# A graph-attention and GraphSAGE kernel: who divides by the softmax sum, when the list decoder's right sides are made, and which queue stores the last row

## The chip, the cores and the metric

The kernel runs on one core of a Trainium2 chip, as one launch. The metric is the device time in microseconds (us) of that launch. Each core has a matrix engine (TensorE, in the profile PE), a vector engine (VectorE, DVE), an activation engine (ScalarE, ACT), GpSimd (POOL) and SyncE (SP). Each has its own queue of instructions, which it works through in order. DMA transfers are issued from the queues of SP, ACT and POOL.

## The reference

The input is a table `x` of 4096 nodes by 512 features and a matrix `adj` of 4096 by 4096 int32, in which about one entry in a thousand is 1. Two layers follow each other, each with a residual sum and a layer norm.

```python
# layer 0: graph attention, 8 heads of 64
Wh = jnp.einsum('nf,hfo->hno', x, W)
f1 = jnp.einsum('hno,ho->hn', Wh, a[:, :F_OUT]);  f2 = ... a[:, F_OUT:]
e = jax.nn.leaky_relu(f1[:, :, None] + f2[:, None, :], ALPHA)
e = jnp.where(adj[None, :, :] > 0, e, NEG_INF)
out = jnp.einsum('hnm,hmo->hno', jax.nn.softmax(e, axis=-1), Wh)
x = _layernorm(x + out)
# layer 1: mean over the neighbours, then three linear maps
agg = (adj > 0) @ x / jnp.maximum(deg, 1.0)
y = concatenate([x @ W_self + b_self, agg @ W_nb + b_nb]) @ W_comb + b_comb
x = _layernorm(x + relu(y))
```

## The kernel before, in words

The 4096 nodes are cut into 32 blocks of 128. Because `adj` is almost empty, the kernel does not multiply by it: it turns each row of `adj` into a short list of neighbour numbers and gathers the neighbours' rows from a table in device memory. (A dense version stands behind a flag and is not entered on this input.)

**Stage 1** (the loop at line 951, counter `b`, and what follows to line 1027). For each block TensorE transposes `x` (`transposed`, line 354) and multiplies it with the weights in two halves (`node_half`, line 375); VectorE copies each half from PSUM into a tile `row` (line 379), and `store` (line 947) writes the row of `Wh`, with its attention terms, to the table `t0`. Rows 0 to 30 are stored from POOL's queue. The last, row 31, is stored at line 980 from ACT's queue, where it stands behind the masks of the last `adj` block (`mask_adj`, line 428). SP's queue carries the loads of `adj` (1 MB each, tile `at`). Behind its last one stands `load_late` (line 928), a load of 1 MB into the tile `m1` for one of the three `adj` blocks that are handled later.

Lists are decoded for four blocks at a time by the generator `decode` (line 464). It yields between pieces, and `some(lists)` runs one piece: four pieces for each `b` in stage 1. Its sixteen pieces are, in order: three of bit work, four of maxima, the count of neighbours (which makes `nx`, line 504), two empty ones, piece 11 with a small product on TensorE (line 511) and the first of four selection matrices (lines 520 and 521), three more of these, piece 15 with the right side `lq` (line 525), the products of the four selections with it (line 531) and all that reads them (lines 535 to 548), and piece 16 with the owner table (line 550).

**Stage 2**, layer 0 (the loop at line 1035, counter `i` from -3 to 33; here "pass i"). It is a pipeline over blocks, written out by hand. Every engine's order is the order of these calls:

- TensorE: `a_shared(i+1)` (line 694, the weighted sums of the gathered rows of block i+1), then a decoder product if a piece has one, `a_z(i-1)` (line 739, block i-1 times a folded weight), `transposed(i)` (line 354), and on some even passes the fold of a late `adj` block (line 447).
- POOL: five row gathers for block i+6 (line 621). There are five gather buffers, so they wait for `a_shared(i+1)`.
- VectorE: `a_weights(i+3)` (lines 652, 653), `a_weigh(i+2)` (line 669, the long one), `a_recip(i+1)` (line 702), `a_first(i+2)` (line 677), `a_own_sum(i+2)` (line 687), the second half of `a_scale(i+1)` (line 710), a piece of the decoder on passes -2 to 4 and from 9 on, `a_moments(i+1)` (line 717, the sum with x).
- ScalarE: `root(i)` and `norm(i)` (lines 725 to 734), the first half of `a_scale(i+1)` (line 708, four operations of 64 columns), `a_exp(i+3)` (lines 659, 660), a cast of owners (line 648), copies of the product of `a_z` (line 743) and of the transposed block (line 360), and on even passes up to 8 the mask of a late half block (line 943), after which SP issues the next load into the single tile `m1`.

Two PSUM facts matter in this stage. The exponentials `ew` have one buffer, so `a_exp(i+3)` waits until `a_own_sum(i+2)` has read the last ones. Decoder products and transposed blocks share one buffer, `tp`.

**Stage 3**, layer 1 (line 1156), gathers rows of a second table `t1`, which `a_z` has filled, and multiplies on TensorE (lines 765 and 772).

Of the kernel before, what the change touches and what calls it, by code (L numbers as in the profile page):

```python
# [36 lines left out]
OP = mybir.AluOpType  # L37
# [3 lines left out]
P = 128  # L41
# [72 lines left out]
def listed_layers(  # L114
# [15 lines left out]
    nc = tc.nc  # L130
    N, FIN = x.shape
    H, _, D = w0.shape
    NB = N // P
    FB = FIN // P
    HD = H * D
    HH = HD // 2
# [327 lines left out]
    def decode(b0, dp, place):  # L464
# [40 lines left out]
        dg = dp.tile([P, G], F32, name="dg", bufs=1)  # L505
        nc.vector.tensor_scalar(dg, deg[:, bs], 1.0, None, OP.max)
        nc.vector.reciprocal(L[:, :, KL + 1], dg)
        for k in range(3):
            yield
        po = ps.tile([P, G], F32, name="sm", bufs=2)  # L510
        nc.tensor.matmul(po, lhsT=triuq, rhs=nx, start=True, stop=True)
# [4 lines left out]
        for b in range(b0, b0 + G):  # L516
# [9 lines left out]
            lq, lst[:, bs, K0:].unsqueeze(2).to_broadcast([P, G, KH, EX + H]),  # L526
            part.unsqueeze(1).unsqueeze(3).to_broadcast([P, G, KH, EX + H]), OP.mult,
        )
        pe = ps.tile([P, G, KH, EX + H], F32, name="sm", bufs=2)
        for g in range(G):  # L530
            nc.tensor.matmul(
# [98 lines left out]
    def gather(table, b, g, at=None):  # L630
        for k in range(KS):
            rows_of(
                g[:, k, 0 : table.shape[1]], table, (idx if at is None else at)[:, b, k : k + 1]
            )
        return g

    def gather_early(b, pool):
        return gather(t1[0 : 2 + min(LE + b, LX) * P, :], b, pool, idxe)
# [5 lines left out]
    G0, OWN, E, RD, Y, NM, MV, RS = ({} for _ in range(8))  # L644

    def a_owners(b, wp):
        OWN[b] = wp.tile([P, KH, HP], F32, name="own", bufs=4)
        nc.scalar.copy(OWN[b], own[:, b])

    def a_weights(b, wp):  # L650
        e = E[b] = wp.tile([P, KS + 1, H], F32, name="e", bufs=3)[:, 0:KS]
        nc.vector.tensor_add(e, G0[b][:, :, 0:H], f1s[:, b])
        nc.vector.scalar_tensor_tensor(e, e, SLOPE, e, OP.mult, OP.max)
# [8 lines left out]
    def halves_of(t):  # L662
        return t[:, H : H + 2 * (2 * HH - H)].rearrange(
            "p (a c) -> p a c", a=2
        )[:, :, 0:HH]

    def a_weigh(b, sl):
        gv = G0[b][:, sl, H:TW].rearrange("p k (h d) -> p k h d", h=H)
        nc.vector.tensor_tensor(  # L669
            gv, gv, E[b][:, sl].unsqueeze(3).to_broadcast([P, sl.stop - sl.start, H, D]),  # L670
            OP.mult,
        )

    def a_first(b):

        NM[b] = ps.tile([P, 2 * HD], F32, name="num")
        nc.vector.tensor_tensor(
            halves_of(NM[b]).rearrange("p a (h d) -> p a h d", d=D),
            G0[b][:, 0, H:TW].rearrange("p (a h d) -> p a h d", a=2, d=D),
            E[b][:, 0].rearrange("p (a h) -> p a h", a=2).unsqueeze(3).to_broadcast(  # L680
                [P, 2, H // 2, D]
            ),
            OP.mult,
        )

    def a_own_sum(b):
        nc.vector.tensor_copy(NM[b][:, 0:H], E[b][:, 0])

    def a_shared(b):

        for a in range(2):
            r = slice(a * (H + HH), H + HH + a * HH)
            for k in range(KH):
                nc.tensor.matmul(  # L694
                    NM[b][ts(k, HP), a * HD : a * HD + r.stop - r.start],
                    lhsT=OWN[b][:, k, :], rhs=G0[b][:, K0 + k, r],
                    start=False, stop=True, tile_position=(0, k * HP), skip_group_check=True,
                )

    def a_recip(b, wp):  # L700
        RD[b] = wp.tile([P, H], F32, name="rd", bufs=2)
        nc.vector.reciprocal(RD[b], NM[b][:, 0:H])  # L702

    def a_scale(b):

        for h in range(H // 2):
            s = NM[b][:, H + h * D : H + (h + 1) * D]
            nc.scalar.mul(s, s, RD[b][:, h : h + 1])  # L708
        s = NM[b][:, HD : HD + HH].rearrange("p (h d) -> p h d", d=D)
        nc.vector.tensor_tensor(  # L710
            s, s, RD[b][:, H // 2 :].unsqueeze(2).to_broadcast([P, H // 2, D]), OP.mult
        )

    def a_moments(b, wp):
        Y[b] = wp.tile([P, HD], F32, name="y", bufs=2)
        mu = MV[b] = small.tile([P, 1], F32, name="ln_sum")
        nc.vector.scalar_tensor_tensor(
            Y[b].rearrange("p (a c) -> p a c", a=2), halves_of(NM[b]), 1.0,
            xs[:, b, :].rearrange("p (a c) -> p a c", a=2), OP.mult, OP.add, accum_out=mu,
        )  # L720

    def root(b, wide):

        rs = RS[b] = small.tile([P, 1], F32, name="ln_rs")
        nc.scalar.activation(  # L725
            wide, Y[b], AF.Square, bias=MV[b], scale=-float(HD), accum_out=rs
        )
        nc.scalar.activation(rs, rs, AF.Ln, bias=eps, scale=1.0 / HD**3)
        nc.scalar.activation(rs, rs, AF.Exp, scale=-0.5)
        nc.scalar.mul(MV[b], MV[b], -1.0 / HD)  # L730
        nc.scalar.mul(MV[b], MV[b], rs)

    def norm(b, to):
        nc.scalar.activation(to, Y[b], AF.Identity, bias=MV[b], scale=RS[b])  # L734
# [71 lines left out]
    def some(todo):  # L806
        for p in todo:
            next(p, None)
# [86 lines left out]
    def node_block(w, xT, between=None, keep=False):  # L895
        row = wp.tile([P, FW], F32, name="row", bufs=3)
        node_half(w, 0, xT, w_sb, row)
        if between is not None:
            fold_adj(between, dp)
            max_keys(between)  # L900
        node_half(w, 1, xT, w_sb, row)
        node_rest(w, row)
        if not keep:
            store(w, row, nc.gpsimd)
        return row
# [17 lines left out]
    def load_late():  # L923

        if late:
            b, h = late[0]
            r = b * P + h * (P // NH)
            nc.sync.dma_start(
                m1.bitcast(I32),
                adj[r : r + P // NH, :].rearrange("(j r) (s c) -> (r s) j c", r=RG, s=SEG),  # L930
            )
# [14 lines left out]
    def store(w, row, eng=nc.scalar):  # L946
        eng.dma_start(t0[2 + w * P : 2 + (w + 1) * P, :], row)

    w, lists = 0, []
    for b in range(LB):  # L950
# [11 lines left out]
        for k in range(1 + (b in AHEAD)):  # L962
# [7 lines left out]
            row = node_block(w, xT, None if k or nxt is None else b, keep=nxt is None)  # L970
            w, xT = w + 1, nxt
# [5 lines left out]
            next(pieces, None)  # L977
        if b % G == G - 1:
            lists = [decode(b + 1 - G, dp, on_own)]
    store(w - 1, row)  # L980
    load_late()
    xa_cm.__exit__(None, None, None)

# [33 lines left out]
    wq = ctx.enter_context(tc.tile_pool(name="work2", bufs=1))  # L1017
# [12 lines left out]
    def on(b):  # L1030
        return 0 <= b < NB
# [3 lines left out]
    for i in range(-3, NB + 2):  # L1035
        if on(i + 1):
            a_shared(i + 1)
        if on(i + 1 + GA):
            G0[i + 1 + GA] = gather(t0, i + 1 + GA, gps[(i + 1 + GA) % GA])
        elif on(i + GA - NB - 1) and i + GA - NB - 1 < GA:  # L1040
            b = i + GA - NB - 1
            G1[b] = gather_early(b, gps[(NB + b) % GA])
        if on(i + 3):
            a_weights(i + 3, wq)
        if on(i + 2):
            a_weigh(i + 2, slice(K0, KS))
        if on(i + 1):
            a_recip(i + 1, wq)
        if on(i + 2):
            a_first(i + 2)  # L1050
            a_own_sum(i + 2)
        if on(i):
            root(i, xs[:, i, :])
            norm(i, xs[:, i, :])
        if on(i + 1):
            a_scale(i + 1)
        if -3 < i <= 4 or i > TURN:
            some(lists)
            if i > TURN and i % 3 == 0:
                some(lists)  # L1060
        if i == 21:
            lists = [late_lists(dp, last)]
        if on(i + 1):
            a_moments(i + 1, wq)
        if on(i + 3):
            a_exp(i + 3)
        if i == -3:
            a_owners(0, wp)
        if on(i + 4):
            a_owners(i + 4, wp)  # L1070
        if i == -3:
            pieces(4, m2s)
        if i == -2:
            for _ in m2s:
                pass
        if on(i - 1):
            a_z(i - 1, XT.pop(i - 1), m2, wp)
        if on(i):
            XT[i] = transposed(i, wp)
            store_xT(i, XT[i])  # L1080
        if i > -3 and i % 2 == 0 and late:
            b, h = late[0]
            mask_late(lp)
            if h:
                key_bank(b)
                fold_adj(b, dp)
                max_keys(b)
        if i == TURN:
            lists = [chain(lists[0], decode(NB - G, dp, on_last))]
        if 2 <= i < 6:  # L1090
            next(biased)
        if i == TURN + 1:
            loaded = load_fold(0, w_self, m1, weight(fc, "wc"))
        if 16 <= i < 20:
            if i == 16:
                biased = fold_bias(loaded, bcol[:, 0:FB])
            next(biased)
        if i == 20:
            sum_bias()
# [479 lines left out]
```

## Time and profile before

| | |
|---|---|
| median of three runs | 668.76 us (667.65 to 668.82) |
| profiled execution | 669.31 us, of it 667.5 us span |
| TensorE busy | 564.3 us, 85% |
| ScalarE busy | 441.0 us, 66% |
| VectorE busy | 402.6 us, 60% |
| GpSimd busy | 353.4 us, 53% |
| mean granted TensorE clock | 0.951 |
| first gather of stage 2 | 214.07 us |
| first neighbour sum of stage 3 | 469.43 us |

The span runs from the first to the last instruction; the profiled execution's own time is 1.8 us longer. Busy shares are averages over three stages with different limits, so they say little alone: stage 1 runs to about 214 us, stage 2 to about 469 us, stage 3 to the end. A row of the list of waits has an engine and its line, what released it, the total in us, the number of times and the longest. A row of the timeline has start and duration in us, engine, line, operation, output and inputs, and in brackets the idle time of that engine before it.

### The profile page before, as it was taken

The page shows a single profiled execution, that of the slowest core. Times are in us where ns is not written, and L with a number is a line of the kernel's source. Part 1 is how long each engine was busy: PE and PEld are TensorE (multiplying, and loading weights), DVE is VectorE, ACT ScalarE, POOL GpSimd, SP SyncE. Part 2 cuts the span into 40 slices and gives each one's busy share as a digit, 9 for nine tenths or more (in the row PEclk, how much of TensorE's full clock was granted, in tenths as well). Part 3 has the DMA queues.
Part 4 walks back from the last instruction along what each step waited for, and adds up shares of the span by engine and source line. Part 5 has one row for each costly group of instructions (what it writes and reads, how often), then busy time and mean ns, then how long its engine had stood idle before and what let it go on. Part 6 is the DMA issues. An engine that isn't in the chain of part 4 may idle for free.

```text
span 667.5 us, 9452 instructions
## 1 busy us (share of the span) xinstructions
PE 564.3 (85%) x2562; PEld 282.4 (42%) x2562; DVE 402.6 (60%) x1214; ACT 441.0 (66%) x1152; POOL 353.4 (53%) x475
## 2 busy tenths in 40 slices
PE   4798889888897728686988679899899999999992
PEld 2466566656664303332433243444343333333320
DVE  7246858686786557676888968886014454454321
ACT  2687879788783247579788748697326566766443
POOL 5112121112113777567577757637776777777770
PEclk9989999999999957789899979999999999999996
DMA  8999999999997789889799979859978899989882
GB/s 250 406 408 408 410 407 408 409 408 400 390 360 282 211 278 322 301 279 345 253 388 316 302 212 301 279 196 299 316 232 279 301 323 315 336 309 327 296 248 101
DMA packets 92070, 210.45 MB, mean 315 GB/s; under 512 B 13726, under 2 KB 13734, under 8 KB 92010
## 3 DMA queue, kind: packets, MB, share of 16 engines
q1 hardware_dynamic: 63024, 114.05, 46.0%
q0 software_dynamic: 28656, 95.18, 44.2%
q10 hardware_dynamic: 330, 0.55, 0.2%
q8 instruction: 23, 0.38, 0.2%
q14 instruction: 37, 0.30, 0.1%
HBM read 175.91 MB, written 33.82 MB: 314 GB/s over the span
## 4 chain that ended last, share of the span: by engine, by line
PE 43%; DMA 23%; ACT 16%; DVE 9%; issue 4%; POOL 3%; SPq 1%; ACTq 0%; DVEq 0%; POOLq 0%
DMA at<-in_adj_dram 14%; PE pw L765 9%; PE nm L765 9%; PE pw L739 5%; PE pw L375 5%; DMA g<-t,idx 5%; PE pw L772 4%; ACT ab L428 4%; PE nm L772 3%; DMA m<-in_adj_dram 3%; ACT num L708 3%; POOL g L621 3%; PE tp L313 2%; DVE g L669 2%; ACT xs L734 2%
## 5 line engine op out<-in xcount | busy, mean ns | idle before, releaser
L621 POOL DMA_INDIRECT g<-t,idx x290 | 275.3, 949 | 115.2 <-issue 48.4
L375 PE MATMUL pw<-w_sb,xT 128*128 128x264 f32 x512 | 130.5, 401 | 6.6 <-issue 3.7
L428 ACT ACTIVATE ab<-at 128x2048 bf16<-128x2048 int32 x58 | 110.9, 1917 | 34.3 <-DMA at<-in_adj_dram 33.5
L739 PE MATMUL pw<-wr,xT 128*128 128x512 f32 x256 | 124.1, 629 | 7.2 <-ACT xT L360 7.1
L375 PEld LDWEIGHTS pw<-w_sb,xT 128*128 128x128 f32 x512 | 94.7, 194 | 33.6 <-issue 9.6
L382 POOL COPY lst<-row 128x8 f32<-128x8 f32 x32 | 8.6, 270 | 158.1 <-DVE row L379 136.6
L739 PEld LDWEIGHTS pw<-wr,xT 128*128 128x128 f32 x256 | 48.5, 200 | 70.1 <-issue 53.1
L669 DVE TENSOR_TENSOR g<-g,ew 128x2048 f32<-128x2048 f32 x32 | 72.9, 2279 | 0.0
L765 PE MATMUL nm<-m,xT 128*128 128x512 f32 x128 | 58.8, 602 | 0.0
L765 PE MATMUL pw<-m,xT 128*128 128x512 f32 x128 | 58.8, 602 | 0.0
L354 PE MATMUL tp<-ident,xs 128*128 128x128 f32 x256 | 40.6, 283 | 11.6 <-ACT xs L734 4.1
L708 ACT ACTIVATE num<-num,rd 128x64 f32<-128x64 f32 x128 | 36.7, 287 | 19.9 <-DVE rd L702 16.5
L379 DVE COPY row<-pw 128x264 f32<-128x264 f32 x64 | 27.2, 426 | 32.6 <-PE pw L375 26.4
L354 PEld LDWEIGHTS tp<-ident,xs 128*128 128x128 f32 x256 | 31.5, 145 | 36.2 <-issue 10.7
L694 PE MATMUL num<-g,own 128*32 128x256 f32 (+1 forms) x512 | 39.4, 420 | 8.3 <-ACT num L708 5.0
L621 POOL DMA_INDIRECT g<-t,idxe x30 | 28.4, 945 | 19.2 <-DMA xt<-xT 9.3
L765 PEld LDWEIGHTS pw<-m,xT 128*128 128x128 f32 x128 | 23.3, 190 | 34.9 <-issue 28.0
L765 PEld LDWEIGHTS nm<-m,xT 128*128 128x128 f32 x128 | 23.3, 190 | 34.9 <-issue 26.5
L788 DVE SCALAR_TENSOR_TENSOR sm<-g,lst,nm 128x512 f32<-128x512 f32 x15 | 11.3, 755 | 42.0 <-PE nm L772 33.8
L725 ACT ACTIVATE row<-y,ln_sum 128x512 f32<-128x512 f32 x32 | 23.1, 722 | 20.0 <-DVE y L793 20.0
L788 DVE SCALAR_TENSOR_TENSOR sm<-g,lst,pw 128x512 f32<-128x512 f32 x15 | 11.3, 755 | 41.1 <-PE pw L772 37.8
L743 ACT COPY row<-pw 128x512 f32<-128x512 f32 x32 | 18.7, 583 | 23.2 <-PE pw L739 23.1
(235 smaller groups left out, 890.5 us busy)
## 6 DMA issues: line engine op xcount, KB each, us to landing
at<-in_adj_dram SPq DMA_DIRECT2D x58, 1024.0 KB, 11.3
xt<-xT SPq DMA_DIRECT2D x32, 256.0 KB, 4.7
t<-row SPq DMA_DIRECT2D x32, 256.0 KB, 4.6
xT<-xt SPq DMA_DIRECT2D x32, 256.0 KB, 5.2
out_dram<-row SPq DMA_DIRECT2D x32, 256.0 KB, 4.2
t<-row POOLq DMA_DIRECT2D x31, 264.0 KB, 5.6
xs<-in_x_dram SPq DMA_DIRECT2D x31, 256.0 KB, 10.5
m<-in_adj_dram SPq DMA_DIRECT2D x6, 1024.0 KB, 10.9
```

Source lines behind the costliest of these rows:

```text
L354: nc.tensor.transpose(tp[:, c, :], xs[:, b, ts(c, P)], ident)
L375: nc.tensor.matmul(pw, lhsT=xT[:, c, :], rhs=w_sb[:, c, k * HW : (k + 1) * HW], start=(c == 0), stop=(c == FB - 1),)
L379: nc.vector.tensor_copy(row[:, k * HW : (k + 1) * HW], pw)
L428: nc.scalar.activation(ab, loads.pop((b, h)), AF.Relu, accum_out=asum[:, b, h : h + 1])
L621: nc.gpsimd.indirect_dma_start(out=out, out_offset=None, in_=table, in_offset=bass.IndirectOffsetOnAxis(ap=at, axis=0),)
L669: nc.vector.tensor_tensor(gv, gv, E[b][:, sl].unsqueeze(3).to_broadcast([P, sl.stop - sl.start, H, D]), OP.mult,)
L694: nc.tensor.matmul(NM[b][ts(k, HP), a * HD : a * HD + r.stop - r.start], lhsT=OWN[b][:, k, :], rhs=G0[b][:, K0 + k, r], start=False, stop= ...
L708: nc.scalar.mul(s, s, RD[b][:, h : h + 1])
L725: nc.scalar.activation(wide, Y[b], AF.Square, bias=MV[b], scale=-float(HD), accum_out=rs)
L739: nc.tensor.matmul(pz, lhsT=xT[:, c, :], rhs=m2[:, c, :], start=(c == 0), stop=(c == FB - 1))
L765: nc.tensor.matmul(NM[b], lhsT=xT[:, c, :], rhs=m1[:, c, :], start=False, stop=(c == FB - 1), skip_group_check=True,)
L772: nc.tensor.matmul(NM[b][ts(k, HP), :], lhsT=OWN[b][:, k, :], rhs=g[:, K0 + k, 0:HD], start=False, stop=True, tile_position=(0, k * HP), s ...
```

## The change

VectorE divides all eight heads by their sums in one operation of 512 columns, from PSUM to PSUM; ScalarE's four operations go. In a pass, this division and the sum with x move ahead of `a_first(i+2)` and `a_own_sum(i+2)` on VectorE. In the decoder one of the empty pieces goes and a new piece boundary stands between `lq` and the products that use it: line 511 and the selections come one piece earlier (pieces 10 to 13), `lq` is piece 14 alone, the products stay in piece 15. Row 31 is stored from SP's queue, where it stands ahead of `load_late`.

```diff
@@ decode
-        for k in range(3):
+        for k in range(2):
             yield
         po = ps.tile([P, G], F32, name="sm", bufs=2)
         nc.tensor.matmul(po, lhsT=triuq, rhs=nx, start=True, stop=True)
...
             part.unsqueeze(1).unsqueeze(3).to_broadcast([P, G, KH, EX + H]), OP.mult,
         )
+        yield
         pe = ps.tile([P, G, KH, EX + H], F32, name="sm", bufs=2)
@@ a_scale
-        for h in range(H // 2):
-            s = NM[b][:, H + h * D : H + (h + 1) * D]
-            nc.scalar.mul(s, s, RD[b][:, h : h + 1])
-        s = NM[b][:, HD : HD + HH].rearrange("p (h d) -> p h d", d=D)
+        s = halves_of(NM[b]).rearrange("p a (h d) -> p a h d", d=D)
         nc.vector.tensor_tensor(
-            s, s, RD[b][:, H // 2 :].unsqueeze(2).to_broadcast([P, H // 2, D]), OP.mult
+            s, s, RD[b].rearrange("p (a h) -> p a h", a=2).unsqueeze(3).to_broadcast(
+                [P, 2, H // 2, D]
+            ), OP.mult,
         )
@@ after the loop of stage 1
-    store(w - 1, row)
+    store(w - 1, row, nc.sync)
     load_late()
@@ the loop of stage 2
         if on(i + 1):
             a_recip(i + 1, wq)
+        if on(i + 1):
+            a_scale(i + 1)
+            a_moments(i + 1, wq)
         if on(i + 2):
             a_first(i + 2)
             a_own_sum(i + 2)
         if on(i):
             root(i, xs[:, i, :])
             norm(i, xs[:, i, :])
-        if on(i + 1):
-            a_scale(i + 1)
         if -3 < i <= 4 or i > TURN:
             some(lists)
...
-        if on(i + 1):
-            a_moments(i + 1, wq)
         if on(i + 3):
             a_exp(i + 3)
```

## The prediction

> **What bounds the kernel now.** I read the page first, then the busy times by stage, then the waits of stage 2, then the timeline where the long waits are. The page says that TensorE leads and holds the largest share of the chain:
>
> ```profile
> PE 564.3 (85%) x2562; PEld 282.4 (42%) x2562; DVE 402.6 (60%) x1214; ACT 441.0 (66%) x1152; POOL 353.4 (53%) x475
> PE 43%; DMA 23%; ACT 16%; DVE 9%; issue 4%; POOL 3%; SPq 1%; ACTq 0%; DVEq 0%; POOLq 0%
> ```
>
> Busy times by stretch of the span (columns: PE, weight loads, DVE, ACT, POOL, clock, DMA):
>
> ```profile
> core 0: us, PE busy (x) PEld busy (x) DVE busy (x) ACT busy (x) POOL busy (x), PEclk, DMA share, GB/s
> 236.00:286.00 50.00, 30.89 (x156) 14.61 (x159) 33.27 (x75) 29.25 (x90) 34.53 (x37) 0.71 0.90 297
> 286.00:320.00 34.00, 26.54 (x153) 11.63 (x146) 22.77 (x52) 28.59 (x79) 20.99 (x22) 0.89 0.96 328
> 320.00:395.00 75.00, 61.66 (x318) 28.68 (x319) 64.94 (x155) 54.17 (x171) 52.63 (x55) 0.94 0.90 299
> 395.00:469.00 74.00, 65.90 (x327) 30.22 (x326) 56.80 (x147) 58.63 (x181) 47.45 (x51) 1.00 0.82 265
> 469.00:668.00 199.00, 183.59 (x574) 64.40 (x574) 72.52 (x214) 104.18 (x266) 137.00 (x145) 0.97 0.84 281
> ```
>
> In stage 3 TensorE is busy 184 of 199 us, and nothing of the change is there. Stage 2 has no single limit: TensorE idles 19 of 50 us at first, VectorE works 65 of 75 us in the middle, ScalarE 59 of 74 at the end. Its waits, in 236 to 466 us:
>
> ```profile
> DVE num L710 <- ACT num L708: 27.6, 32, 3.2
> ...
> PE tp L531 <- DVE lq L525: 13.8, 2, 7.4
> ...
> PE pw L447 <- ACT abl L943: 11.7, 3, 6.3
> ...
> PE pw L739 <- ACT xT L360: 7.1, 10, 0.9
> ```
>
> Two waits of TensorE for `lq` cost 13.8 us. VectorE waits for ScalarE's half of the division in every block, 27.6 us in 32 times. The second wait for `lq`, in pass 19:
>
> ```profile
> 378.17 1.08 PE L694 MATMUL num<-g,own 128*32 128x264 f32 x16 [0.23 <-DVE num L687]
> ...
> 385.97 0.58 DVE L525 TENSOR_TENSOR lq<-lst,part 128x416 f32<-128x416 f32 x1
> 386.70 2.00 PE L531 MATMUL tp<-lq,last 128*128 128x104 f32 x8 [7.44 <-DVE lq L525]
> 388.49 4.87 PE L739 MATMUL pw<-wr,xT 128*128 128x512 f32 x8
> ```
>
> TensorE had all else that it needed and stood still. Last, the way into stage 2:
>
> ```profile
> 205.56 0.43 DVE L379 COPY row<-pw 128x264 f32<-128x264 f32 x1 [1.29 <-PE pw L375]
> 209.44 0.35 ACTq L947 DMA_DIRECT2D t<-row  x1
> 214.07 1.05 POOL L621 DMA_INDIRECT g<-t,idx  x1 [7.28 <-PE key L447]
> ```
>
> Row 31 is ready at 205.99, is issued 3.45 us later behind a mask on ACT, lands 3.8 us after that (the DMA view), and the first gather follows.
>
> **What the Trainium skill says.** "VectorE: DVE Perf Modes", section "Mode 1× (REGULAR) — the baseline", gives one result a cycle for an fp32 operation on two tensors, PSUM operands too, at the 0.96 GHz of its "Specifications": 256 more columns should take 0.27 us. The trace agrees: 512 columns took 0.67 us (line 677), 256 took 0.43 (line 710). "TensorE: Matmul & The Clock Gate", section "What's actually happening", says that an idle window of some 3.4 us halves the clock and that about as long a busy one restores it. The trace agrees: the eight matmuls of line 739 took 4.87 us after the 7.44 us wait, 3.70 otherwise. "DMA: Bandwidth & Descriptors", section "Queues, rings and completion order", says that SP and ACT each own one row of rings on the same 16 engines, consumed in ring order. So row 31 on SP goes behind the last `adj` loads, which land at 209.38. No run here shows it.
>
> **Row 31 and the stage-1 pieces.** On SP the store needs no mask to end: 3.45 us less. The same edit of the decoder costs some of it. Line 511 now stands ahead of the block's transposes, and TensorE waits there for `nx`; behind it in TensorE's queue stands the whole next block. For b=18, `nx` ended at 142.12 and TensorE was there at 138.64: 3.5 us, hidden by the `adj` loads that the chain shows from 136.16 to 146.81. For b=22: 172.22 against 169.67, 2.6 us; of it line 531's wait for `lq` (1.02) and a wait behind the selections (0.97) are repaid, leaving about 0.4. For b=26: 196.82 against 194.93, 1.9 us with no repayment before row 31. So row 31 is ready at about 208.3, lands 3.8 later, and with the same 0.8 us to the first gather I get 212.9 instead of 214.07. The `m1` load behind it on SP moves from 197.16 to about 209; its reader started at 233.66 and the slowest such load took 10.96, so that costs nothing; were the cover gone, the mask would be late by the rest. ACT loses one issue of 0.35 us.
>
> **The order on VectorE.** Before: reciprocal to the end of `a_own_sum` takes 0.12 + 0.71 + 0.17 (starts to starts), then 0.52 of waiting where it is shortest, then 0.34 and 0.69 for half the division and the sum with x: 2.55. After, with about 0.1 for each of two new waits on its own last result: 0.24 + 0.75 + 0.69 + 0.71 + 0.17 = 2.56. VectorE's own round is thus no shorter where it waited only 0.52, but `a_own_sum(i+2)` ends 1.5 us later in it. Behind it wait `a_shared(i+2)` on TensorE and, for the single `ew` buffer, `a_exp(i+3)` on ScalarE, with the cast, both copies and the mask queued behind. ScalarE's round falls by 1.25, from about 5.75 (1.8 root, 0.8 norm, 1.25, 0.43, 0.28, two copies 1.16) to 4.5.
>
> **Along the stage, by the start of a block's products (line 694):**
>
> 1. Block 2: 253.16 before. The gathers start 1.2 earlier, but the mask ahead of the fold now waits for the later `a_own_sum`: **-0.5**.
> 2. Block 5: 280.70 before. `lq` is ready a pass early; TensorE saves its 6.4 us wait and some 1.4 us of slow clock (5.1 against 3.7 us for line 739). Next late is the shared `tp` buffer: the transposes must wait until VectorE has read the products (line 545), by my count at about 272. So **-7.5** for this wait.
> 3. Block 10: 317.60 before. On passes 4 and 8 the fold waits for ScalarE's mask, itself behind `a_exp` and the `m1` load (10.96 us): **+2** given back.
> 4. Block 20: 378.17 before. VectorE sets the pace of 6.2 to 6.3 us, with 6.25 for five gathers (5 x 1.25) close behind; 0 to 0.2 longer a pass over ten: **+2**, the upper end taken.
> 5. Block 22: 400.69 before, 19.1 after VectorE began pass 19 (381.56). After: pass 19 loses its 2.19 us wait for the products and takes 8.0, then 5.1 and TensorE's sum of biases to block 22: 13.5; `lq` in pass 18 adds 0.4. **-5.2**.
> 6. To block 31 and the last `a_z`: 5.9 us a pass before, near ScalarE's 5.75; TensorE's own 5.1 is the floor, and late lists and VectorE's 5.1 stand close: **-3.5** over nine passes.
>
> The sum is -12.7. Against the profiled execution that is 669.3 - 12.7 = 656.6; it ran 0.55 above the median, so the median falls from 668.76 to about **656**.
>
> **Unknown costs.** The 512-column division from PSUM to PSUM is not in the trace: at least 0.67 (line 677), at most two of line 710, 0.86; I take 0.70. Over 30 blocks the ends differ by 6 us if VectorE sets every pass. The store on SP: 0 gain if the `adj` backlog holds it, 3.5 at best. The wait at line 511: 0 to 4.5 us. Even without one stall the gathers end 160 x 1.25 = 200 us after their start, 20 us sooner than the 432.3 of now, so a gain much past 25 us is excluded.
>
> **Rivals.**
> - *More*: ScalarE was the true limit of stage 2. For it: 59 of 74 us busy, VectorE's 27.6 us of waits. Against: in the middle VectorE is busier. Items 3 and 4 vanish and item 6 doubles: -20, **648**.
> - *Less*: the wait for `lq` turns into one for `tp`, since both decoder products and transposes use it, and VectorE stays the pace. Then only its own two waits of 2.19 and the start are won, with 2 to 3 at the end: -6 to -8, **662**.
> - *Slower*: the later `a_own_sum`. If the single `ew` buffer decides in nearly every pass, each of 32 passes gains the mean VectorE wait of 0.86 and loses 1.5: +20, against -13.8 for `lq`, -3 for ScalarE's load and nothing at the start: +3, **672**. It decides from the point where ScalarE has finished its norm before `a_own_sum` ends. Against: on TensorE's round the products come last, not `ew`.
> - *The pieces do nothing*: line 531 could still find `lq` late. Against: `lq` would stand a whole pass, 6 us, earlier in VectorE's queue.
>
> **The numbers.** Forecast 55%, more 12%, less 18%, slower 12%, no change 3%. Differences within 0.2% (1.3 us) can't be told from none. The range 645 to 667 takes in forecast, more and less with the bounds above.
>
> **What would show it.** Right: line 531 no longer waits for line 525; line 710's wait is gone and the 128x512 division takes about 0.70; the first gather comes at 211 to 214; block 5 at about 273, block 22 near 389; the last `a_z` 10 to 15 us sooner; stage 3 as long as now. Wrong: line 354 waits long for line 545, or line 694 for line 687, or line 659 for line 687 in most passes.

## The result, and the profile after

The change makes the kernel faster by 1.1%: 662.03 us median of four runs (658.63 to 662.90) against 668.56 us for the kernel before in the same session, ratio 0.9886 with a 95% interval of 0.9845 to 0.9927. The forecast was 656.0. The profiled execution below is the fastest of the four, 658.63 us with a span of 656.9. One run of this study (658.90 us, of the change with its order turned) counts as slow, being over 1.5% above the fastest of its kernel, and is left out of that kernel's ratio.

The two page lines that answer those of before, engine totals and chain shares:

```profile
PE 561.8 (86%) x2562; PEld 283.7 (43%) x2562; DVE 414.7 (63%) x1214; ACT 406.2 (62%) x1024; POOL 353.4 (54%) x475
PE 50%; DVE 21%; DMA 17%; ACT 4%; issue 3%; POOL 3%; SPq 1%; DVEq 0%; ACTq 0%; POOLq 0%
```

ScalarE lost 35 us of work and 128 instructions, VectorE gained 12 us. On the chain ScalarE fell from 16% to 4%, and VectorE rose from 9% to 21%. Busy times by stretch of stage 2 and of stage 3 (columns as before):

```profile
core 0: us, PE busy (x) PEld busy (x) DVE busy (x) ACT busy (x) POOL busy (x), PEclk, DMA share, GB/s
236.00:280.00 44.00, 28.68 (x166) 12.84 (x159) 35.71 (x77) 24.44 (x67) 33.33 (x36) 0.81 0.93 315
...
320.00:384.00 64.00, 54.30 (x290) 24.81 (x289) 61.81 (x139) 39.58 (x120) 46.95 (x50) 0.97 0.95 324
384.00:458.00 74.00, 67.96 (x326) 31.44 (x324) 61.73 (x148) 46.24 (x133) 48.50 (x51) 0.95 0.83 272
458.00:657.00 199.00, 183.07 (x574) 64.50 (x574) 72.21 (x214) 104.40 (x266) 136.22 (x145) 0.97 0.84 280
```

In the middle VectorE now works 61.8 of 64 us: it is the pace there. At the end ScalarE's load fell from 58.6 to 46.2 of 74 us, yet the stretch is as long as it was. Stage 3 is unchanged. The waits of stage 2 (total, times, longest):

```profile
ACT ew L660 <- DVE num L688: 64.3, 28, 6.1
...
PE pw L447 <- ACT abl L943: 12.4, 3, 7.0
...
PE num L695 <- DVE num L688: 6.9, 7, 1.6
...
PE tp L354 <- DVE jk L546: 3.4, 2, 2.0
```

The waits for `lq` (13.8 us) and for ScalarE's half of the division (27.6 us) are gone. In their place stand two new ones for `a_own_sum` (line 688), of ScalarE and of TensorE, and a small one for the shared `tp` buffer. TensorE around the decoder product of pass 19:

```profile
374.81 1.14 PE L532 MATMUL tp<-lq,last 128*128 128x104 f32 x8 [0.48 <-ACT xT L360]
375.78 3.62 PE L739 MATMUL pw<-wr,xT 128*128 128x512 f32 x8
381.41 0.63 PE L354 MATMUL tp<-ident,xs 128*128 128x128 f32 x4 [2.01 <-DVE jk L546]
```

The 7.44 us wait is now 0.48, the eight matmuls of line 739 take 3.62 us instead of 4.87, and the next thing late is `tp`, 2.01 us. The way into stage 2:

```profile
199.39 0.16 PE L511 MATMUL sm<-nx,triuq 128*128 128x4 bf16 x1 [1.88 <-DVE nx L504]
...
210.02 0.43 DVE L379 COPY row<-pw 128x264 f32<-128x264 f32 x1 [1.29 <-PE pw L375]
210.48 0.34 SPq L947 DMA_DIRECT2D t<-row  x1
214.18 1.05 POOL L622 DMA_INDIRECT g<-t,idx  x1 [3.23 <-DMA t<-row]
```

Row 31 is issued 0.03 us after it is ready, but it is ready at 210.45 instead of 205.99. The store's earlier issue was spent: the first gather is at 214.18, against 214.07 before.

### The profile page after: what moved, and what is told of

It reads as the page before. It is cut to its first block, busy times and chain, and to the rows that moved or that the text cites. A ratio compares the mean times of both kernels' runs of the same rounds, so it can differ in the third digit from the quotient of the medians.

```text
span 656.9 us, 9327 instructions
## 1 busy us (share of the span) xinstructions
PE 561.8 (86%) x2562; PEld 283.7 (43%) x2562; DVE 414.7 (63%) x1214; ACT 406.2 (62%) x1024; POOL 353.4 (54%) x475
## 4 chain that ended last, share of the span: by engine, by line
PE 50%; DVE 21%; DMA 17%; ACT 4%; issue 3%; POOL 3%; SPq 1%; DVEq 0%; ACTq 0%; POOLq 0%
PE pw L375 12%; PE nm L765 9%; PE pw L765 9%; DMA g<-t,idx 8%; PE pw L739 5%; DVE g L670 5%; PE pw L772 4%; DMA at<-in_adj_dram 3%; PE nm L772 3%; POOL g L622 3%; PE tp L313 2%; DMA m<-in_adj_dram 2%; PE tp L354 2%; DVE num L708 1%; DVE y L717 1%
## 5 line engine op out<-in xcount | busy, mean ns | idle before, releaser
L375 PE MATMUL pw<-w_sb,xT 128*128 128x264 f32 x512 | 133.5, 408 | 6.1 <-issue 3.8
L375 PEld LDWEIGHTS pw<-w_sb,xT 128*128 128x128 f32 x512 | 96.8, 198 | 33.4 <-issue 13.1
L382 POOL COPY lst<-row 128x8 f32<-128x8 f32 x32 | 6.9, 215 | 163.7 <-DVE row L379 163.7
L695 PE MATMUL num<-g,own 128*32 128x256 f32 (+1 forms) x512 | 37.2, 404 | 12.4 <-DVE num L688 6.9
L660 ACT ACTIVATE ew<-e 128x40 f32<-128x40 f32 x32 | 6.6, 207 | 64.5 <-DVE num L688 64.3
L367 ACT ACTIVATE xT<-tp 128x128 f32<-128x128 f32 x100 | 26.3, 287 | 23.2 <-PE tp L354 23.2
```

The lines of the kernel that those rows point to most:

```text
L367: nc.scalar.activation(t[:, c, :], tp[:, c, :], AF.Copy, accum_out=sums[:, c, b : b + 1])
L375: nc.tensor.matmul(pw, lhsT=xT[:, c, :], rhs=w_sb[:, c, k * HW : (k + 1) * HW], start=(c == 0), stop=(c == FB - 1),)
L695: nc.tensor.matmul(NM[b][ts(k, HP), a * HD : a * HD + r.stop - r.start], lhsT=OWN[b][:, k, :], rhs=G0[b][:, K0 + k, r], start=False, stop= ...
```

## Experiments

All were timed in five rounds. The median of the kernel before was 668.79, 669.84 and 668.30 us in the three sets. Landmarks (first gather, start of a block's products) are those of the profiled execution of each kernel.

### The parts alone

The first set runs the change again and each of its three parts on the kernel before: the decoder's pieces (`range(2)` and the new `yield`), the division with the order on VectorE, and the store from SP.

> The changed kernel once more, beside the three parts on the same chip, so that its distance to the kernel before and their sum can be compared. Expected 659 to 663 us, 6 to 8 below before. The first gather of stage 2 near 214, block 5 near 274, block 20 near 373, the last product of line 739 near 454.

> The decoder's pieces alone; division and last store as before. Theory A (the waits for lq were the price, and the pieces pay for most of the change): row 31 comes about 4 us later, since TensorE waits at line 511 for nx in four-block groups (3.4, 3.4, 2.4 and 1.9 us), then stage 2 wins 7 at pass 3 and 5 to 7 at pass 19: 5 to 9 us below before. Theory B (the division is what pays, and VectorE's own pace hides lq's place): the waits at line 531 move to line 354, and with the later row 31 the kernel is 0 to 4 us slower than before.

> The division by VectorE and the order alone; decoder's pieces and last store as before. Theory A: VectorE's round is as long as before (2.56 against 2.55 us from reciprocal to the end of the sum with x), the exponentials come 1.5 us later, so -1 to +4 us. Theory B: VectorE loses 27.6 us of waiting for ScalarE, and the kernel gets 6 to 12 us faster.

> The last row's store on SP's queue alone. If the store was held only by ScalarE's queue: it is issued near 206.1, lands some 3.5 us sooner, the first gather comes at 210.5 to 211.5 instead of 214.07, and 1 to 3.5 us are won in the end. If the loads of adj ahead of it in SP's rings hold it: it lands after 211.5 and less than 1 us is won.

| kernel | median us (lowest to highest) | ratio, 95% interval | row 31 ready | first gather | first gather to block 31 |
|---|---|---|---|---|---|
| before (the first profile) | 668.79 | | 205.99 | 214.07 | 239.6 |
| the change again | 664.25 (657.32 to 666.13) | 0.9909, 0.9871 to 0.9946 | 213.91 | 217.06 | 234.1 |
| pieces alone | 661.16 (657.57 to 664.82) | 0.9900, 0.9862 to 0.9938 | 207.17 | 213.30 | 230.7 |
| division and order alone | 670.91 (666.55 to 674.23) | 1.0026, 1.0009 to 1.0043 | 206.22 | 214.45 | 238.4 |
| store alone | 665.42 (661.64 to 667.88) | 0.9953, 0.9939 to 0.9968 | 205.84 | 210.96 | 238.7 |

The pieces bring 1.0%, the store 0.5%, and the division costs 0.3%. Their sum, 1.2%, lies within the intervals of the whole. Each part's time came out as its first expectation had it. The repeat came 1.3 us above the top of its expectation, its first gather at 217.06 and not near 214. Taking 1.25 us a block off ScalarE bought nothing in this order on VectorE. And the kernels with line 511 at the earlier place have row 31 at 207.2, 210.5 and 213.9, where the others have 205.8 to 206.2: they are later and they scatter.

### The cut at a later place

If the early line 511 is what delays row 31, the same effect for `lq` must be had without it. Here `lq` has its own piece as in the change, line 511 stays in piece 11, and two selections share its piece. The store is on SP in both kernels of this kind; the first has the division of before, the second that of the change with its order.

```diff
-        for k in range(2):
+        for k in range(3):
...
-            yield
+            if b > b0:
+                yield
```

> Division as before, row 31 stored by SP; in the decoder lq is a piece of its own ahead of its products, but line 511 stays in piece 11 (two selections share that piece, so there are sixteen still). Theory A (the early line 511 costs stage 1 its time, the early lq wins stage 2): no wait at line 511, row 31 near 206, first gather near 211, from there to block 31's products 230 us as in the run of the pieces alone, so 653 to 656 us, 2.0 to 2.4% below before. Theory B (line 511 costs nothing, row 31 came later for another reason): first gather near 214, 658 to 661 us.

> The run before it with the division by VectorE and the order of the change. Theory A (VectorE is the pace in most of stage 2 and its round is as long either way): within 3 us of the run before it, 653 to 659 us. Theory B (the division wins time once lq is early, since ScalarE is the next limit): 4 us or more below the run before it.

Measured: 654.79 us (654.43 to 658.01), ratio 0.9791 (0.9768 to 0.9814), with the division of before, and 655.94 us (654.25 to 657.86), ratio 0.9789 (0.9768 to 0.9809), with that of the change. So the place of line 511, with the selections that follow it, cost the change 6 to 8 us. The gain of the pieces is kept: from the first gather to block 22 it is 174.7 and 178.1 us, 176.1 in the change and 180.4 in its repeat, 186.6 before. The two ways of dividing differ by about 1 us of median, within their intervals. The end of stage 1, first in the change, then with the cut at the later place and the division of before. The lines are the last two `adj` loads on SP's queue, the mask that waits for the last of them, and the first gather:

```profile
194.72 6.37 SPq L422 DMA_DIRECT2D at<-in_adj_dram  x2
...
212.77 1.91 ACT L428 ACTIVATE ab<-at 128x2048 bf16<-128x2048 int32 x1 [1.31 <-DMA at<-in_adj_dram]
214.18 1.05 POOL L622 DMA_INDIRECT g<-t,idx  x1 [3.23 <-DMA t<-row]
```

```profile
189.89 6.88 SPq L422 DMA_DIRECT2D at<-in_adj_dram  x2
...
197.70 0.17 PE L511 MATMUL sm<-nx,triuq 128*128 128x4 bf16 x1
...
209.33 1.91 ACT L428 ACTIVATE ab<-at 128x2048 bf16<-128x2048 int32 x1 [0.53 <-DMA at<-in_adj_dram]
210.82 1.05 POOL L623 DMA_INDIRECT g<-t,idx  x1 [6.35 <-DMA t<-row]
```

The mask begins when the last `adj` load has landed. With the later cut TensorE has no wait at line 511, row 31 is ready at 203.96, 6.5 us sooner than in the change, but its gather starts only 3.4 us sooner. In ten of the eleven profiled kernels of this study that store from SP, the first gather comes 1.41 to 1.53 us after the last `adj` load has landed, wherever between 203.4 and 211.1 the row was ready. In the eleventh, the repeat of the change with its row at 213.91, it is 1.88. So where the row is early, the store ends with the `adj` loads ahead of it on SP. Where the row is late, the store's own way counts too: the gather comes 3.12 and 3.13 us after the store's issue in the two kernels with the latest rows (213.91 and 211.06), 3.70 us in the profiled change, and 5.1 to 6.8 us in the others. The Trainium skill's statement on rings ("DMA: Bandwidth & Descriptors", "Queues, rings and completion order"), which no run had shown when the prediction was made, agrees with this. Whether the order in SP's ring holds the store, or only the load on the 16 engines that all queues share, no run tells apart.

### The later `a_own_sum`

The rival "slower" rested on the order on VectorE. Here `a_first(i+2)` and `a_own_sum(i+2)` go back ahead of the division and the sum with x, once with the later cut and once in the change itself.

```diff
-        if on(i + 1):
-            a_scale(i + 1)
-            a_moments(i + 1, wq)
         if on(i + 2):
             a_first(i + 2)
             a_own_sum(i + 2)
+        if on(i + 1):
+            a_scale(i + 1)
+            a_moments(i + 1, wq)
```

> As the run before it, but a_first and a_own_sum stand ahead of the division and the sum with x again. If the later a_own_sum is what eats the gain (exponentials, copies and mask on ScalarE wait for it): ScalarE's wait of line 660 for line 688 shrinks from 64 us to under 25 us, and 2 to 5 us are won. If only VectorE's whole round counts: the wait shrinks as much and the time stays within 1.5 us.

> The change as it is, with only the order on VectorE turned: a_first(i+2) and a_own_sum(i+2) ahead of the division and the sum with x. Theory S (the late a_own_sum holds ScalarE at the single ew buffer, as with the later pieces, where the same turn gave 8.7 us): 653 to 656 us against 662 to 664 for the change, ScalarE's wait for a_own_sum from 64 down to about 40 us. Rival (the early line 511 and its late row 31 set the end, the order only shifts waits): 660 us or more.

Measured: with the later cut 647.22 us (644.83 to 649.07), ratio 0.9666 (0.9641 to 0.9691), 8.7 us below the same kernel in the change's order. That is more than the 2 to 5 us expected, though ScalarE's wait fell only to 39.9 us and not under 25. In the change itself it is 652.56 us (648.11 to 658.90; 650.89 without the highest), ratio 0.9746 (0.9702 to 0.9790), by the ratios some 9 to 11 us below the change. The order is the largest single item found, and it goes against the change.

It also hid what the division is worth. Beside the kernel with the later cut and the division of before (654.79), 647.22 is 7.6 us less: VectorE's division, with the sum with x right behind it, does pay once `a_own_sum` comes first. In the change's order that gain was spent, so the division looked worth nothing. (No run has the division on VectorE with the sum with x at its old place, so these two are not separated.) The waits for `a_own_sum`, in the change's order and then turned (later cut, both):

```profile
ACT ew L661 <- DVE num L689: 63.4, 27, 5.9
...
PE num L696 <- DVE num L689: 7.7, 8, 1.6
```

```profile
ACT ew L661 <- DVE num L689: 39.9, 23, 3.6
...
PE num L696 <- DVE num L689: 1.7, 3, 0.8
```

VectorE's round itself also became shorter. One round near the end, in the change and then with its order turned:

```profile
423.99 0.20 DVE L703 RECIPROCAL rd<-num 128x8 f32<-128x8 f32 x1
...
424.22 0.70 DVE L708 TENSOR_TENSOR num<-num,rd 128x512 f32<-128x512 f32 x1
...
424.96 0.69 DVE L717 SCALAR_TENSOR_TENSOR y<-num,xs 128x512 f32<-128x512 f32 x1
...
425.57 0.69 DVE L678 TENSOR_TENSOR num<-g,ew 128x512 f32<-128x512 f32 x1
...
426.30 0.17 DVE L688 COPY num<-ew 128x8 f32<-128x8 f32 x1
426.51 0.20 DVE L653 TENSOR_TENSOR e<-g,f1s 128x40 f32<-128x40 f32 x1
```

```profile
421.62 0.20 DVE L703 RECIPROCAL rd<-num 128x8 f32<-128x8 f32 x1
421.74 0.67 DVE L678 TENSOR_TENSOR num<-g,ew 128x512 f32<-128x512 f32 x1
...
422.44 0.17 DVE L688 COPY num<-ew 128x8 f32<-128x8 f32 x1
422.53 0.69 DVE L708 TENSOR_TENSOR num<-num,rd 128x512 f32<-128x512 f32 x1
...
423.25 0.69 DVE L717 SCALAR_TENSOR_TENSOR y<-num,xs 128x512 f32<-128x512 f32 x1
...
423.87 0.19 DVE L653 TENSOR_TENSOR e<-g,f1s 128x40 f32<-128x40 f32 x1
```

From the reciprocal to the next block's first operation it is 2.52 us and 2.25 us. The division needs the reciprocal's result and starts 0.23 us after it; line 678, which doesn't, starts after 0.12. Behind the copy of line 688 it is 0.21 and 0.09, for another reason, since neither line 653 nor line 708 needs the copy's result. Line 653 waits for the gathers of its block, and the trace has two instructions of VectorE's queue for that wait between the copy and line 653:

```profile
L653 DVEq EVENT_SEMAPHORE  x2: 49/50/50, 426.3 to 426.4; - x2
```

In the turned order they pass while the 0.69 us of the sum with x run (423.3 to 423.4). Where an operation of the decoder stood behind the copy in the change, it started after 0.08 us, but for two that waited for TensorE. From start to start of line 670, rounds without a decoder piece and without a gap take 5.07 to 5.09 us in the change and 4.79 turned. Four successive rounds with decoder pieces in the middle of the stage (5.95, 5.80, 6.59 and 5.80 us in the change) are each 0.13 to 0.19 shorter turned.

### Is it the single `ew` buffer?

> As the second run of this group, but the exponentials ew are in three buffers in SBUF instead of one in PSUM, so that line 660 needs no a_own_sum. If the single buffer decides: 2 to 6 us below the second run. If VectorE's round decides: the wait of ScalarE for line 688 goes to near nothing and the time stays within 1.5 us of the second run.

> late_divide with its single ew buffer in SBUF instead of PSUM: one buffer as before, only the place differs. Theory H (a gather issued while VectorE reads two inputs from SBUF, as the multiplication of line 671 then does, is held up for the length of that operation): gathers of line 623 mean 1.2 to 1.3 us, some of 3 us, and 680 to 700 us. Rival (three buffers let other work run so early that it collided with the gathers): gathers at 0.95 to 1.0 us and 654 to 660 us.

> late_divide (the change with pieces cut at the later place), but the exponentials alternate between two halves of one PSUM tile. Theory S: the single ew buffer is what the later a_own_sum costs, so ScalarE's wait for it (63 us) goes and the time comes to that of late_sum_first, 645 to 650 us, with gathers at their 0.95 us. Rival P: what cost the 8.7 us is TensorE's wait for a_own_sum (7.7 us in late_divide, 1.7 in late_sum_first), since the products add onto its tile: 654 to 656 us. If PSUM tiles are tracked whole, the wait stays and so does the time, 656 us.

> late_sum_first with the exponentials in two halves of one PSUM tile. If ScalarE's remaining 40 us of waits for a_own_sum still cost time: 640 to 644 us. If VectorE is the pace by then (it works 57 of 59 us in the middle of the stage and 36 of 37 after it): 645 to 649 us, ScalarE's wait turned into another.

```diff
@@ three buffers in SBUF
-        w = E[b] = ps.tile([P, KS, H], F32, name="ew")
+        w = E[b] = small.tile([P, KS, H], F32, name="ew", bufs=3)
@@ one buffer in SBUF
+        w = E[b] = small.tile([P, KS, H], F32, name="ew", bufs=1)
@@ two halves of one PSUM tile
+        w = E[b] = EW[:, b % 2]
```

With three buffers in SBUF the wait of ScalarE for line 689 is gone, and the kernel takes 689.33 us (686.98 to 691.85), ratio 1.0284 (1.0258 to 1.0311). With one buffer in SBUF it takes 689.59 us (685.58 to 691.31), ratio 1.0304 (1.0266 to 1.0342), with 84.5 us of that wait in 236 to 440 us. So the place of the tile costs 33 us, whatever the number of buffers. The groups of the gathers in 236 to 440 us, `ew` in PSUM and then one buffer in SBUF:

```profile
L623 POOL DMA_INDIRECT g<-t,idx x141 | 135.2, 959 | 50.8 <-issue 28.1 <-ACT xs L735 5.7 <-DMA g<-t,idx 4.6
```

```profile
L623 POOL DMA_INDIRECT g<-t,idx x129 | 165.7, 1284 | 39.3 <-issue 18.3 <-DMA g<-t,idx 7.0 <-PE num L696 3.4
```

A gather issued while VectorE multiplies (line 671), in the same two kernels:

```profile
342.12 2.28 DVE L671 TENSOR_TENSOR g<-g,ew 128x2048 f32<-128x2048 f32 x1
342.35 0.95 POOL L623 DMA_INDIRECT g<-t,idx  x1 [0.30 <-PE num L696]
```

```profile
340.11 2.28 DVE L671 TENSOR_TENSOR g<-g,ew 128x2048 f32<-128x2048 f32 x1
340.70 2.51 POOL L623 DMA_INDIRECT g<-t,idx  x1 [0.30 <-issue]
```

With `ew` in PSUM the gather takes 0.95 us beside the multiplication. With `ew` in SBUF both inputs of line 671 come from SBUF, and the gather takes 2.51 us and ends 0.82 us after the multiplication does. The test of the buffer is thus spoilt by its place.

The halves of one PSUM tile came out at 657.10 us (653.30 to 659.17), ratio 0.9824 (0.9787 to 0.9860), in the change's order and at 646.43 us (643.59 to 649.48), ratio 0.9672 (0.9637 to 0.9706), in the turned one, with ScalarE's wait for line 689 as long as before, 66.4 and 41.8 us. The wait stayed, as the last branch of the expectation has it for a tile that is tracked whole, so they test nothing of the buffer. They do repeat their two parents (655.94 and 647.22) within 1.2 us, and show the order to be worth 10.7 us once more.

## Why the prediction was right, and where not

The direction and the largest item were right; the size was 6 us too large. Against the profiled pair the steps read:

| step | predicted | measured | the repeat |
|---|---|---|---|
| first gather | 212.9 (from 214.07) | 214.18 | 217.06 |
| 1: products of block 2 | -0.5 in all | +1.0 in all | +4.8 in all |
| 2: to block 5 | -7.5 | -7.3 | -7.4 |
| 3: to block 10 | +2 | -0.5 | +3.1 |
| 4: to block 20 | +2 | +1.9 | +1.7 |
| 5: to block 22 | -5.2 | -5.5 | -5.5 |
| 6: to the last `a_z` | -3.5 | -0.3 | +0.7 |

- **The pieces** (steps 2 and 5) worked as written: both waits for `lq` went with the slow matmuls behind them, and `tp` was late next. Alone on the kernel before they bring 7.6 us of median.
- **The start failed in its mechanism and its size.** The prediction took row 31 at 208.3 plus a landing of 3.8, with the wait at b = 18 hidden and that at b = 22 nearly repaid. The row came at 210.5 and 213.9. All four profiles with the early line 511 show waits there of 14 to 16 us, in six pieces of stage 1 (1.9 to 3.4 us each), and their rows are 1.2, 4.5, 5.1 and 7.9 us later than before. So most of the waits is hidden, but not a fixed part of it: at row 20 (b = 20) the change is already 1.3 us behind the kernel before and its repeat 3.3, while the pieces alone are 1.0 ahead. What decides this stays open. The bound of "0 to 4.5 us" was too low for the repeat. The last `adj` load landed at 212.8 instead of 209.4 as well, having been issued some 4 us later. The prediction had named that backlog, and had taken its end in the kernel before as fixed. In the profiled change it added some 0.6 us by this measure (3.70 us from issue to gather, against 3.12), so there the late row is what counts.
- **The division** cost nothing to speak of, as forecast: 512 columns from PSUM to PSUM took 0.70 us, and VectorE's round 2.52 for 2.56 predicted. That it brings nothing held only with the order that the change gives VectorE. That VectorE is the pace in the middle (step 4) was right to 0.3 us in both profiles.
- **Step 3** expected the fold's wait to give back 2 us. In the profiled pair nothing was given back (TensorE's waits for the mask came to 12.4 us after 11.7). In the repeat they came to 17.4, and 3.1 us were lost, by the path that the prediction named: ScalarE's mask waited for the `m1` load, and the fold for the mask. The two lines are from the repeat; in the change the same wait of the fold was 2.08 us.

```profile
315.67 1.91 ACT L943 ACTIVATE abl<-m 128x2048 bf16<-128x2048 int32 x1 [3.18 <-DMA m<-in_adj_dram]
...
317.72 0.61 PE L447 MATMUL pw<-abl,fold 128*32 128x512 bf16 x2 [5.37 <-ACT abl L943]
```

- **The tail (step 6) was read from a mean and a sum.** ScalarE's 5.75 us is a sum of durations that overlap. Where it works without idle time before, its round is 5.14 us from start to start:

```profile
439.23 0.74 ACT L725 ACTIVATE xs<-y,ln_sum 128x512 f32<-128x512 f32 x1
...
444.37 0.74 ACT L725 ACTIVATE xs<-y,ln_sum 128x512 f32<-128x512 f32 x1
```

The 5.9 us a pass is a mean of unlike passes. The five from the products of block 26 to those of block 31 take 9.53, 5.08, 5.82, 5.14 and 5.08 us before, 10.34 and four times 5.08 after: 30.66 us both times. TensorE's own round is 5.08. So less work on ScalarE was worth at most 0.8 us there, in two passes. The pass to block 27, with pieces of the late lists, got as much longer; that the sums are equal is chance. In that pass VectorE's rounds of 6.6 to 7.8 us are the same in both kernels, and in the profiled change eight matmuls of line 739 took 6.59 us instead of 3.68, with a granted clock of 0.61 in 416 to 423 us (1.00 in 421 to 432 us before). In the repeat they took 3.68, and the five passes 30.32.
- **The rival "slower"** named a real cost, the later `a_own_sum`, at 8.7 to 11 us instead of its estimate of 20. One of the prediction's signs of being wrong came: ScalarE's exponentials wait for `a_own_sum` 28 times, in most passes. The forecast had compared VectorE's round only with that of before. Against the same operations in the other order it is 0.27 us longer, and ScalarE's and TensorE's waits come on top. The traces tell the two apart. Without VectorE's idle stretches of over 0.15 us, its 31 rounds together are 5.4 to 5.5 us shorter when the order is turned, in all three pairs (the change, the later cut, the two halves in PSUM). The idle stretches shrink by 4.6 and 3.8 us in the two pairs with the later cut, so there the waits are somewhat under half of what the order costs. In the pair of the change they grow by 1.6, with one late fold in the turned run, so the start of stage 3 moves only from 458.63 to 454.80 there. Whether a second `ew` buffer would save the waits stays open: one in PSUM that is tracked by itself was not tried.

The median, 662.0, is the number of the rival "less", but not for its reason. Steps 2 and 5 gave what the forecast said, and TensorE waits for `tp` only 3.4 us in two times. The start, the tail and the order took back the rest.

The profiled pair has to be read beside the medians: the thirteen runs of the change lie between 657.2 and 666.1 us, and the profiled 658.6 is the third lowest of them. Its steps sum to -10.8 us, where the medians moved by 6.5 and 4.5. The profiled repeat (666.1) shows what varies: its last `a_z` begins 8.3 us later, 3.8 of them by block 2, 3.5 in step 3 and 1.1 in step 6. Steps 2, 4 and 5 agree within 0.2 us.

The best kernels run have all of the change but the place of line 511 and the order on VectorE: 646.4 to 647.2 us, 3.3% below the kernel before.

## What to carry to other kernels

When a generator's pieces are recut, look at what its first matrix product waits for in the stage that runs it most often, and not only at the stage that the cut is meant for: in an in-order queue a small product placed early holds everything behind it while it waits. A wait that ends on one transfer can be held by another ahead of it in the same queue, so ask what moves that one too. When an engine is about to become the pace, write its operations so that the result that other engines wait for comes first, that one that makes a small result is followed by one that doesn't need it, and that one with several waits of its own stands behind a long one. And when two edits are made at once, try each with the other undone: here the order of two operations hid what the division was worth.

## What the runs showed of the hardware that was not expected

A gather issued from GpSimd's queue is held up while VectorE runs an operation with both inputs in SBUF. With `ew` in SBUF, 26 of 26 gathers that began inside line 671 in 230 to 440 us ended 0.81 to 0.82 us after it and took 2.06 to 3.06 us. With `ew` in PSUM, all 54 such gathers took 0.94 or 0.95 us. The Trainium skill ("SBUF — State Buffer", "Who interferes with whom") says that a VectorE instruction with two SBUF inputs contends with a GpSimd instruction that reads SBUF, that the port pair which the two share is an exclusive lock, and that the order of issue decides which of them is blocked; these numbers agree. VectorE's multiplication kept its 2.28 us throughout. The place of a tile of 40 columns thus cost 33 us of 656.
